# Softmax row sums of an attention layer: from products with ones on TensorE to a pass through DRAM, GpSimd additions and VectorE block transposes

## The chip, the cores and the metric

The kernel runs on one core of a Trainium2 chip. The time is the device time of one execution in microseconds (us). A core has five engines that run side by side, each taking its own instructions strictly in order: TensorE (PE, matmuls into PSUM), VectorE (DVE), ScalarE (ACT), GpSimd (POOL) and SyncE (SP), which here only issues transfers (DMA). PEld is PE's loading of weights.

## The reference

Two graph layers, each with a layer norm and a ReLU ahead and a residual around it, on 64 batches of 256 tokens with 512 features, in float32. The change concerns the second one, masked attention with 8 heads of 64:

```python
q = split_heads(h @ Wq.T + bq)
k = split_heads(h @ Wk.T + bk)
v = split_heads(h @ Wv.T + bv)
scores = jnp.einsum('bhqd,bhkd->bhqk', q, k) * scale
scores = jnp.where(mask, -jnp.inf, scores)
attn = jax.nn.softmax(scores, axis=-1)
out = jnp.einsum('bhqk,bhkd->bhqd', attn, v)
out = out.transpose(0, 2, 1, 3).reshape(b, n, D_MODEL)
return out @ Wo.T + bo
```

The first layer is a graph attention with one head: `e` is a sum of a column and a row term, goes through a leaky ReLU, the mask and a softmax, and weighs `h = X W`; its output is the weighted `h` beside `h` itself.

## The kernel before

The 64 batches are worked in 32 groups `g` of two batches `b`. All programs are unrolled Python loops. A software pipeline interleaves four things: the attention of batch (g,b), the output product of the batch before it, the q, k and v products of group g+1, and the first layer and norms of groups g+2 and g+3. One turn of this pipeline is called a stage (g,b) here.

The main loop (line 940 on) reads the order of each stage from a string. `S` issues the scores, `m` masks one pair of heads, `u` takes a piece of the projections of g+1 (`project`), `o` a piece of the output product (`outputs`), `s` a piece of the first layer (`first_layer`), `n` a piece of the first norm (`first_norm`). Each stage starts with `weigh`, which finishes the batch before, and then with `scores`.

PE's matmuls are held in exactly the order in which the program writes them (`in_order`, line 131). On the other engines a scheduler may move instructions, except that `not_sooner` (line 123) puts one behind the last one that was recorded on its engine. An engine then works in that fixed order: an instruction that waits holds up all behind it.

The steps around the change:

- `scores` (line 755): per head two matmuls per 128 keys into a PSUM bank, then ACT's exponential into `p` (128 keys by head, key half and 256 queries). The banks come from a ring of five (`mm`, line 109), which `ph`, `po`, `pr`, `total` and others share.
- `mask_pairs` (line 780): DVE multiplies a pair of heads by the mask; POOL then adds the second key half into the first, `p[:, :, 0, :] += p[:, :, 1, :]`, so that sums over keys need one half only.
- `value_differences` (line 750): POOL subtracts in `v` the first key half from the second, which makes up for that addition in the product with `v`.
- `weigh` (line 799): PE multiplies ones by `p` into `total`: for each query the sum over keys, 4 heads in the 4 blocks of 32 partitions, each block holding 32 equal rows. DVE takes the reciprocal `r`. PE multiplies `v` by `p` into `pr`, one bank for four heads, and DVE writes `oT = pr * r`. DVE then makes sums of the parts of `oT` for a seven-product (Strassen-like) form of the output product.
- `outputs` (line 836): seven products `py`, each added into `x` by DVE. Three use one bank held for them, the rest the ring.
- `project` (line 675): the same seven products for q, k and v; ACT keeps some results (`kept_q`, `kept_k`, `kept_v`) before PE adds to the same bank, DVE adds others.
- `first_layer` (line 552): `ph` matmuls, ACT's copy to `H`, POOL's addition into `x`; a row passed through DRAM (`rows`, `line`, `own`); `e` by ACT, DVE and ACT again; the mask; `po` matmuls, DVE's normalising, the statistics (`stats`: `st`, `mv`) and the norm of the second layer.
- `norm_T` (line 414): the factors of a norm (DVE, then POOL's power), ACT's `xn`, DVE's 32x32 block transposes `xt`, a transfer to DRAM (`passed`) and four back (`moved`), and ACT's copy to `hT`. It is a transposition by DVE's blocks and a trip through DRAM.
- `residual` (line 658): POOL adds the output bias into `x`.

All transfers of the loop are issued on SP. The tiles `p`, `r` and `e` lie in one pool; `p` and `r` have one buffer, `e` has two; `hT0` has one.

Of the kernel before, what the change touches and what calls it, by code (L numbers as in the profile page):

```python
# [57 lines left out]
def bounded(  # L58
# [350 lines left out]
            vector.bn_stats(st, src[t])  # L409
        vector.bn_aggr(mv[:, t, :], st)  # L410

    put_last, sums_last = [], []

    def norm_T(src, mv, name, by_pe):

        factor, xn, passed, turned = {}, {}, {}, {}
        J = P // S  # L420

        def factors(b):
            tiles = slice(b * NT, (b + 1) * NT)
            several = small.tile([P, 3, NT], F32, tag="factor", name=f"factor{name}_{b}")
            ve, less, rstd = (several[:, i, :] for i in range(3))
            vector.tensor_scalar(ve, mv[:, tiles, 1], EPS, None, op0=ALU.add)
            vector.tensor_scalar(less, mv[:, tiles, 0], -1.0, None, op0=ALU.mult)
            if name == "0_0":
                not_sooner(gpsimd, "tensor_tensor", rstd, ve, rexp, op=ALU.pow)
            else:  # L430
                gpsimd.tensor_tensor(rstd, ve, rexp, op=ALU.pow)
            gpsimd.tensor_tensor(less, less, rstd, op=ALU.mult)
            factor[b] = less, rstd

        def norm(b):
            less, rstd = factor[b]
            for t in range(NT):
                r = b * NT + t
                xn[r] = att.tile([P, D], F32, tag="xn", name=f"xn{name}_{r}", bufs=2)
                operands = dict(bias=less[:, t : t + 1], scale=rstd[:, t : t + 1])  # L440
                if scalar.last:
                    last = scalar.last
                    taken = scalar.activation(xn[r], src[r], AF.Relu, **operands)
                    for other in [last, *put_last] if name == "0_2" else [last]:
                        after(taken, other)
                else:
                    scalar.activation(xn[r], src[r], AF.Relu, **operands)

        def turn(b):
            tiles = range(b * NT, (b + 1) * NT)  # L450
            if by_pe:
                for t in tiles:
                    turned[t] = mm(f"pt{name}_{t}").rearrange("p (c n) -> p c n", c=HP)
                    for c in range(HP):
                        transpose(turned[t][:, c, :], xn[t][:, c * P : (c + 1) * P], ident)
                return

            xt = att.tile([P, J, HP, NT, S], F32, tag="xt", name=f"xt{name}_{b}", bufs=1)
            passed[b] = dram.tile([P, J, HP * NT * S], F32, tag="passed", name=f"passed{name}_{b}")
            for t in tiles:  # L460
                not_sooner(
                    vector, "transpose",
                    xt[:, :, :, t % NT, :], xn[t].rearrange("p (c j a) -> p j c a", j=J, a=S),
                )
            sync.dma_start(passed[b], xt.rearrange("p j c t n -> p j (c t n)"))

        def fetch(b):
            if by_pe:
                return
            moved = att.tile([P, J, HP, NT, S], F32, tag="moved", name=f"moved{name}_{b}")  # L470
            for j in range(J):
                nc.sync.dma_start(  # L472
                    moved[j * S : (j + 1) * S].rearrange("a i c t n -> a i (c t n)"),
                    passed[b].rearrange("(i a) j e -> j a i e", a=S)[j],
                )
            for t in range(NT):
                turned[b * NT + t] = moved[:, :, :, t, :].rearrange("p i c n -> p c i n")

        def put(b, dst):
            for t in range(NT):  # L480
                to = dst[:, :, t * P : (t + 1) * P]
                if not by_pe:
                    to = to.rearrange("p c (i n) -> p c i n", n=S)
                not_sooner(scalar, "copy", to, turned[b * NT + t])
            put_last[:] = [scalar.last]

        return factors, norm, turn, fetch, put
# [64 lines left out]
    def first_layer(g):  # L552

        xt = [xs[g, b][:, t, :] for b in range(GB) for t in range(NT)]
        for r in range(GT):
            b, t = divmod(r, NT)
            ph = mm(f"ph_{g}_{r}")[:, : F1 + 2]
            for c in range(HP):
                matmul(
                    ph, hT0[g, b][:, c, t * P : (t + 1) * P], w0_sb[:, c, :],  # L560
                    start=(c == 0), stop=(c == HP - 1),
                )
            scalar.copy(H[:, r, : F1 + 2], ph)
            gpsimd.tensor_add(xt[r][:, F1:], H[:, r, 2 : F1 + 2], xt[r][:, F1:])
            if r < GT - 1:
                yield

        pT = {}
        if g:

            rows = small.tile([P, GT, 8], F32, tag="rows", name=f"rows_{g}", bufs=2)
            not_sooner(vector, "transpose", rows.rearrange("p t c -> p (t c)"), H[:, :, 0:8])
            line = dram.tile([P // 8, S], F32, tag="line", name=f"line_{g}")
            nc.sync.dma_start(line, rows.rearrange("p t c -> p (t c)")[::8, :])
            own = att.tile([P, P // S, GT, S], F32, tag="r", name=f"own_{g}", bufs=1)
            nc.sync.dma_start(
                own.rearrange("p k t j -> p (k t j)"),
                line.rearrange("(o k) j -> o (k j)", o=1).to_broadcast([P, TOK]),
            )
            own = own.rearrange("p k t j -> p t k j")  # L580
            yield
        else:
            yield
            pn = mm(f"pn_{g}")
            for t in range(GT):
                transpose(pn[:, t * P : (t + 1) * P], H[:, t, 0:1].to_broadcast([P, P]), ident)
            own = pn.rearrange("p (t k j) -> p t k j", t=GT, j=S)
        for b in range(GB):
            e = pT[b] = att.tile([P, NT, N], F32, tag="e", name=f"e_{g}_{b}")
            for kb in range(NT):  # L590
                not_sooner(
                    scalar, "activation",
                    e[:, kb, :].rearrange("p (t k j) -> p t k j", t=NT, j=S),
                    own[:, b * NT : (b + 1) * NT], AF.Identity,
                    bias=H[:, b * NT + kb, 1:2], scale=1.0,
                )
# [158 lines left out]
    def scores(g, b):  # L755
# [6 lines left out]
        for i in range(HP):  # L762
# [9 lines left out]
            for j in range(2):  # L772
                last = scalar.last
                made = scalar.activation(pair[:, j], sc[j], AF.Exp, scale=scale)
                for other in [last, *put_last] if g == b == 0 and i > 1 else [last]:
                    after(made, other)
        places.extend((q_tag, k_tag))
        return p
# [1 line left out]
    def mask_pairs(p, last_group):  # L780


        for i in range(HP):
# [10 lines left out]
                after(made, other)  # L794
            yield

    oTs = {}

    def weigh(g, b, p):
# [1 line left out]

        v, v_tag = qkv["v", g, b]
        name = f"{g}_{b}"
        total = mm(f"total_{name}").rearrange("p (q n) -> p q n", q=NQ)
        r = att.tile([P, NQ, N], F32, tag="r", name=f"r_{name}", bufs=1)
        for quad in range(NQ):
            blocks = range(1 if g < NG - 1 else NT)
            for kb in blocks:
                for j in range(QH):
                    matmul(  # L810
                        total[j * S : (j + 1) * S, quad, :], ones, p[:, quad * QH + j, kb, :],
                        start=(kb == 0), stop=(kb == blocks[-1]),
                    )
        for quad in range(NQ):
            not_sooner(vector, "reciprocal", r[:, quad, :], total[:, quad, :])
        for quad in range(NQ):
            pr = mm(f"pr_{name}_{quad}").rearrange("p (h n) -> p h n", h=2)
            for half in range(2):
# [17 lines left out]
    def outputs(g, b):  # L836
# [41 lines left out]
        if g == NG - 1:  # L878
            nc.sync.dma_start(og[g, b][:, 0, D // 2 :], xt[:, 0, D // 2 :])
        else:  # L880
            nc.sync.dma_start(og[g, b], xt)
        yield


# [52 lines left out]
    run(verdict)  # L937


    steps = ("Smmnuuuumonmuossnuussounounonosuo", "Ssmmususuososmuomssusuonusonuouunous")  # L940
    waiting, late = None, iter(())
    for g in range(NG):
        products = project(g + 1) if g + 1 < NG else iter(())
        pieces = first_layer(g + 2) if g + 2 < NG else iter(())
        for b, parts in enumerate(steps):
            if g == b == 0:

                parts = "Smmnnuuuumnnmussnussuunununsu"
            elif g == 0 or g == 1 and b == 0:

                parts = "Ssmmususuososmuomssusuonusouuouous" if b else "Snn" + parts[1:]
            if waiting is not None:
                weigh(*waiting)
                late = outputs(*waiting[:2])
            for i, part in enumerate(parts):
                if part == "u":
                    next(products, None)
                elif part == "o":
# [4 lines left out]
                    next(norms, None)  # L963
                elif part == "m":
                    next(masks)
                else:
                    waiting = (g, b, scores(g, b))
                    masks = mask_pairs(waiting[2], g == NG - 1)
                if i == (len(parts) * 3 // 4, 6)[b] and g < NG - 1:
                    value_differences(g, b)  # L970
                if i == len(parts) // 2:
                    if g == b == 0:
                        weight_sums("o")
                    if g == max(NG - 2, 0) and b == 1:
# [380 lines left out]
```

## Time and profile before

| | |
|---|---|
| median of three runs | 2475.68 us (2475.18 to 2477.83) |
| span of the profiled execution | 2476.3 us |
| POOL's `p` additions | 248 of 1623 ns |
| DVE's mask products `p` | 256 of 1342 ns |
| DVE's reciprocals `r<-total` | 128 of 1727 ns |
| PE's `total<-p,ones` | 1056 records of 128x32 weights, 256 columns |
| granted TensorE clock | 0.999 |
| DMA | 213.58 MB, 26% of 16 engines' time |

The span is that of one profiled execution; the median comes from runs beside it. Busy time is the sum over an engine's instructions; PE's records overlap, since matmuls are pipelined, so that the mean of one is longer than the time it adds. Each float32 matmul leaves two records.

A line of the timeline gives start and duration in us, engine, line of the code (35 is the helper that records every instruction, 137 the matmul helper), operation, output and inputs, shapes and count; in brackets stands the idle time of the engine just before, and what ended it.

### The profile page before, as it was taken

The numbers are of one execution on the slowest core, as the hardware profiler recorded it, in microseconds if no ns is written. First come the engines' busy times: TensorE is split into PE (matmuls) and PEld (weight loads), VectorE is DVE, ScalarE is ACT, GpSimd is POOL, SyncE is SP. The second block draws the span as 40 slices with busy tenths as digits, with TensorE's granted clock in tenths as the row PEclk, the third lists the DMA queues.
The fourth block names the chain that finished last, engine by engine and source line by source line (L and its number), as shares of the span: only waits on it lengthen the run. The fifth ranks groups of instructions, "written<-read, shape, count | busy, mean of one in ns | idle before, by whom it ended". The sixth has DMA issues, their size and how long they took to land.

```text
span 2476.3 us, 41327 instructions
## 1 busy us (share of the span) xinstructions
PE 2453.9 (99%) x16044; PEld 2037.4 (82%) x16044; DVE 1690.3 (68%) x3006; ACT 1010.0 (41%) x2017; POOL 1000.8 (40%) x964
## 2 busy tenths in 40 slices
PE   8999999999999999999999999999999999999998
PEld 7788888888888888888888888888888888888886
DVE  6677666676766776666767667676677666676656
ACT  4544344443443444444434434444434344343431
POOL 2533444433444334444334453344443344433430
PEclk9999999999999999999999999999999999999999
DMA  6222223232232322232322323222222223232100
GB/s 191 77 86 79 84 81 99 86 103 78 72 99 81 103 79 84 82 99 86 99 77 73 103 81 103 79 84 82 94 90 93 78 73 107 80 105 80 52 32 36
DMA packets 135129, 213.58 MB, mean 86 GB/s; under 512 B 15504, under 2 KB 80272, under 8 KB 134928
## 3 DMA queue, kind: packets, MB, share of 16 engines
q1 hardware_dynamic: 134928, 210.89, 26.3%
q8 instruction: 128, 2.10, 0.4%
q14 instruction: 73, 0.60, 0.1%
HBM read 112.20 MB, written 98.63 MB: 85 GB/s over the span
## 4 chain that ended last, share of the span: by engine, by line
PE 97%; DMA 1%; DVE 1%; ACT 0%; issue 0%; SPq 0%; POOL 0%; DVEq 0%
PE pq L137 16%; PE pk L137 16%; PE py L137 15%; PE pv L137 15%; PE sc L137 10%; PE ph L137 9%; PE pr L137 9%; PE po L137 4%; PE total L137 3%; DMA w_sb<-in_L_gnn_W_dram 0%; DMA moved<-passed 0%; DMA passed<-xt 0%; DVE p L35 0%; SPq L472 0%; DVE r L35 0%
## 5 line engine op out<-in xcount | busy, mean ns | idle before, releaser
L35 POOL TENSOR_TENSOR p<-p 128x512 f32<-128x512 f32 x248 | 398.9, 1623 | 676.6 <-DVE p L35 675.3
L35 ACT ACTIVATE p<-sc 128x512 f32<-128x512 f32 x512 | 258.0, 624 | 236.5 <-PE sc L137 232.6
L35 DVE TENSOR_TENSOR p<-p,maskT 128x1024 f32<-128x1024 f32 x256 | 338.3, 1342 | 1.2 <-ACT p L35 1.2
L35 DVE TENSOR_TENSOR x<-py,x 128x256 f32<-128x256 f32 x448 | 186.4, 416 | 166.5 <-PE py L137 157.7
L35 ACT ACTIVATE xn<-x,factor 128x512 f32<-128x512 f32 x256 | 194.5, 808 | 211.4 <-POOL factor L35 211.3
L35 DVE RECIPROCAL r<-total 128x256 f32<-128x256 f32 x128 | 215.7, 1727 | 91.7 <-PE total L137 91.7
L137 PE MATMUL py<-wo_sb,oT 128*128 128x256 f32 x1024 | 262.5, 379 | 0.9 <-DVE oT L35 0.6
L137 PE MATMUL sc<-q,k 64*128 64x256 f32 x2048 | 252.2, 388 | 1.0 <-ACT p L35 1.0
L137 PEld LDWEIGHTS sc<-q,k 64*128 64x128 f32 x2048 | 211.2, 186 | 42.5 <-issue 26.3
L137 PE MATMUL pk<-hT,wk_sb 128*128 128x256 f32 x1024 | 244.8, 382 | 0.0
L137 PE MATMUL pq<-hT,wq_sb 128*128 128x256 f32 x1024 | 239.9, 382 | 0.0
L137 PE MATMUL ph<-w_sb,hT 128*128 128x258 f32 x1024 | 236.8, 384 | 1.5 <-DVE prod L35 1.2
L137 PE MATMUL pv<-wv_sb,hT 128*128 128x256 f32 x1024 | 237.0, 379 | 0.4 <-ACT kept_v L35 0.4
L35 POOL TENSOR_TENSOR factor<-factor,rexp 128x2 f32<-128x2 f32 x128 | 90.6, 708 | 353.9 <-DVE factor L35 353.9
L137 PE MATMUL pr<-p,v 128*32 128x256 f32 x4096 | 232.7, 379 | 0.0
L137 PEld LDWEIGHTS ph<-w_sb,hT 128*128 128x128 f32 x1024 | 195.2, 191 | 32.6 <-ACT hT L35 2.3
L137 PEld LDWEIGHTS pk<-hT,wk_sb 128*128 128x128 f32 x1024 | 192.3, 190 | 35.5 <-issue 10.4
L137 PEld LDWEIGHTS pq<-hT,wq_sb 128*128 128x128 f32 x1024 | 191.8, 190 | 35.3 <-issue 9.9
L137 PEld LDWEIGHTS py<-wo_sb,oT 128*128 128x128 f32 x1024 | 194.1, 190 | 28.9 <-DVE oT L35 1.1
L137 PEld LDWEIGHTS pv<-wv_sb,hT 128*128 128x128 f32 x1024 | 194.4, 190 | 27.2 <-ACT kept_v L35 0.8
L137 PEld LDWEIGHTS pr<-p,v 128*32 128x32 f32 x4096 | 133.1, 110 | 87.9
L137 PE MATMUL py<-wo_sb,o_sums 128*128 128x256 f32 x768 | 197.4, 379 | 0.9 <-DVE x L35 0.9
(125 smaller groups left out, 3637.0 us busy)
## 6 DMA issues: line engine op xcount, KB each, us to landing
passed<-xt SPq DMA_DIRECT2D x124, 512.0 KB, 2.7
moved<-passed SPq DMA_DIRECT2D x496, 128.0 KB, 3.1
x<-in_x_dram SPq DMA_DIRECT2D x64, 512.0 KB, 4.2
out_dram<-x SPq DMA_DIRECT2D x62, 512.0 KB, 3.1
own<-line SPq DMA_DIRECT2D x31, 256.0 KB, 3.1
wq_sb<-in_L_gnn_Wq_dram SPq DMA_DIRECT2D x2, 512.0 KB, 9.8
wk_sb<-in_L_gnn_Wk_dram SPq DMA_DIRECT2D x2, 512.0 KB, 11.0
wv_sb<-in_L_gnn_Wv_dram SPq DMA_DIRECT2D x2, 512.0 KB, 7.4
```

What stands on the lines that cost most here:

```text
L35: instruction = getattr(self.engine, operation)(*args, **kwargs)
L137: in_order(nc.tensor.matmul(*args, **kwargs))
```

## The change

The sums over keys no longer come from PE. For all groups but the last, a new generator `fold` does them in six pieces, called by a new letter `f` in the strings:

1. the first four heads of `p` (first key half, into which POOL has added the second) are written to DRAM (`put`), and read back so that each block of 32 partitions holds one head (`fetch`: four transfers; partition a of the block gets keys a, 32+a, 64+a, 96+a),
2. the second four heads are written to DRAM,
3. POOL adds the four keys of a partition in two additions,
4. DVE transposes the 32x32 blocks and sums each block's 32 keys (`sum_up`); the second four heads are read back,
5. POOL's additions for these,
6. DVE's transposes and sum for these, and a reciprocal of the 16 sums in each partition.

`weigh` then spreads the reciprocals back over partitions with one block transpose of a broadcast input. The read-back data `parts` borrows the buffer of `e` (for b = 0) or of `hT0` (for b = 1); the two `e` tiles of a group become one tile `both` of the same size. In the strings of b = 1 some `m` stand earlier. A few instructions are held behind others (`not_sooner`, `norm_last`) that were free before.

```diff
-    put_last, sums_last = [], []
+    put_last, norm_last, sums_last = [], [], []
...
                     scalar.activation(xn[r], src[r], AF.Relu, **operands)
+            norm_last[:] = [scalar.last]
...
-                nc.sync.dma_start(
+                sync.dma_start(
                     moved[j * S : (j + 1) * S].rearrange("a i c t n -> a i (c t n)"),
...
-            gpsimd.tensor_add(xt[r][:, F1:], H[:, r, 2 : F1 + 2], xt[r][:, F1:])
+            if g < 2:
+                gpsimd.tensor_add(xt[r][:, F1:], H[:, r, 2 : F1 + 2], xt[r][:, F1:])
+            else:
+                not_sooner(
+                    gpsimd, "tensor_add", xt[r][:, F1:], H[:, r, 2 : F1 + 2], xt[r][:, F1:]
+                )
...
+        both = att.tile([P, GB, NT, N], F32, tag="e", name=f"e_{g}", bufs=1)
         for b in range(GB):
-            e = pT[b] = att.tile([P, NT, N], F32, tag="e", name=f"e_{g}_{b}")
+            e = pT[b] = both[:, b]
...
-                for other in [last, *put_last] if g == b == 0 and i > 1 else [last]:
+                if g == b == 0:
+                    others = [last, *put_last] if i > 1 else [last]
+                else:
+                    others = [last, *put_last, *norm_last]
+                for other in others:
                     after(made, other)
...
+    row_sums = {}
+
+    def fold(g, b, p):
+        if g == NG - 1:
+            return
+        compact = small.tile([P, NQ, N // S], F32, tag="compact", name=f"compact_{g}_{b}", bufs=2)
+        row_sums[g, b] = compact
+        pool, tag = (att, "e") if b == 0 else (big, "hT0")
+        rows = []
+
+        def put(quad):
+            rows.append(dram.tile([P, QH, N], F32, tag="rows", name=f"rows_{g}_{b}_{quad}"))
+            heads = slice(quad * QH, (quad + 1) * QH)
+            not_sooner(sync, "dma_start", rows[quad], p[:, heads, 0, :])
+
+        def fetch(quad):
+            parts = pool.tile([P, P // S, N], F32, tag=tag, name=f"parts_{g}_{b}_{quad}", bufs=1)
+            for j in range(QH):
+                not_sooner(
+                    sync, "dma_start", parts[j * S : (j + 1) * S],
+                    rows[quad][:, j, :].rearrange("(i a) n -> a i n", a=S),
+                )
+            return parts
+
+        def add(parts):
+            not_sooner(gpsimd, "tensor_add", parts[:, :2], parts[:, :2], parts[:, 2:])
+            gpsimd.tensor_add(parts[:, 0], parts[:, 0], parts[:, 1])
+
+        def sum_up(quad, parts):
+            not_sooner(vector, "transpose", parts[:, 1], parts[:, 0])
+            vector.reduce_sum(
+                compact[:, quad], parts[:, 1].rearrange("p (k a) -> p k a", a=S), axis=AX.X
+            )
+
+        put(0)
+        parts = fetch(0)
+        yield
+        put(1)
+        yield
+        add(parts)
+        yield
+        sum_up(0, parts)
+        parts = fetch(1)
+        yield
+        add(parts)
+        yield
+        sum_up(1, parts)
+        vector.reciprocal(compact, compact)
+        yield
...
-        total = mm(f"total_{name}").rearrange("p (q n) -> p q n", q=NQ)
         r = att.tile([P, NQ, N], F32, tag="r", name=f"r_{name}", bufs=1)
-        for quad in range(NQ):
-            blocks = range(1 if g < NG - 1 else NT)
-            for kb in blocks:
-                for j in range(QH):
-                    matmul(
-                        total[j * S : (j + 1) * S, quad, :], ones, p[:, quad * QH + j, kb, :],
-                        start=(kb == 0), stop=(kb == blocks[-1]),
-                    )
-        for quad in range(NQ):
-            not_sooner(vector, "reciprocal", r[:, quad, :], total[:, quad, :])
+        if (g, b) in row_sums:
+            compact = row_sums.pop((g, b)).rearrange("p q k -> p (q k)")
+            not_sooner(
+                vector, "transpose", r.rearrange("p q (k a) -> p (q k) a", a=S),
+                compact[:, :, None].to_broadcast([P, NQ * N // S, S]),
+            )
+        else:
...
-            nc.sync.dma_start(og[g, b], xt)
+            not_sooner(sync, "dma_start", og[g, b], xt)
...
-    steps = ("Smmnuuuumonmuossnuussounounonosuo", "Ssmmususuososmuomssusuonusonuouunous")
+    steps = ("Smmfnuuuumonmfuofssfnuufssoufnounonosuo", "Ssmmfusmusmfuososfuosfsusuonufsonufouunous")
...
-                parts = "Smmnnuuuumnnmussnussuunununsu"
+                parts = "Smmfnnuuuumnnmfufssfnussfuununfunsu"
...
-                parts = "Ssmmususuososmuomssusuonusouuouous" if b else "Snn" + parts[1:]
+                parts = "Ssmmfusmusmfuososfuosfsusuonufsoufuouous" if b else "Snn" + parts[1:]
...
+                elif part == "f":
+                    next(folds, None)
+                    continue
                 else:
                     waiting = (g, b, scores(g, b))
                     masks = mask_pairs(waiting[2], g == NG - 1)
+                    folds = fold(*waiting)
```

The branch behind the last `else` of `weigh` is the code of before, for the last group. Positions in a string that start other work (the value differences, the residual, the loads) are counted without the `f`.

## The prediction

> **What bounds the kernel now.** I read the page's busy shares and its chain that ended last, then the chain in order of time for one group of two batches, then the timeline where TensorE (PE) meets the other engines.
>
> ```profile
> PE 2453.9 (99%) x16044; PEld 2037.4 (82%) x16044; DVE 1690.3 (68%) x3006; ACT 1010.0 (41%) x2017; POOL 1000.8 (40%) x964
> ...
> PE 97%; DMA 1%; DVE 1%; ACT 0%; issue 0%; SPq 0%; POOL 0%; DVEq 0%
> ```
>
> PE is never without work, so only PE's own work and new PE waits change the time. The chain in order of time at a stage's start:
>
> ```profile
> 1072.27 1.00 PE total L137 x16
> 1073.27 3.45 PE pr L137 x64
> 1076.72 3.85 PE sc L137 x32
> ```
>
> `total`, the products with ones, costs 1.00 us and follows without a gap. A stage (g,1) lasts 37.0 us (1035.26 to 1072.27), a stage (g,0) 38.8 (1072.20 to 1110.98 in the timeline). The timeline at the end of stage (g,0) shows how early the others are:
>
> ```profile
> 1102.80 0.69 DVE L35 BATCH_NORM_STATS2 st<-x 128x6 f32<-128x512 f32 x1
> ...
> 1104.78 0.71 POOL L35 TENSOR_TENSOR factor<-factor,rexp 128x2 f32<-128x2 f32 x1 [2.10 <-DVE factor L35]
> ...
> 1105.72 1.28 POOL L35 TENSOR_TENSOR v<-v 128x512 f32<-128x512 f32 x1
> ...
> 1106.84 0.69 DVE L35 TENSOR_TENSOR k<-pk,kept_k 128x512 f32<-128x512 f32 x1 [1.37 <-PE pk L137]
> ...
> 1109.50 1.27 DVE L35 SCALAR_TENSOR_TENSOR e<-e 128x512 f32<-128x512 f32 x2
> ...
> 1110.98 1.07 PE L137 MATMUL total<-p,ones 128*32 128x256 f32 x16
> ...
> 1111.87 3.64 PE L137 MATMUL pr<-p,v 128*32 128x256 f32 x64
> 1112.12 3.37 DVE L35 RECIPROCAL r<-total 128x256 f32<-128x256 f32 x2 [0.61 <-PE total L137]
> ...
> 1115.41 1.22 DVE L35 TENSOR_TENSOR oT<-pr,r 128x512 f32<-128x512 f32 x2
> ...
> 1116.60 4.03 ACT L35 ACTIVATE p<-sc 128x512 f32<-128x512 f32 x8 [4.50 <-PE sc L137]
> ```
>
> The statistics (`st`) start 8.2 us before PE's `total`; POOL's `v` difference, which `pr` reads, ends at 1107.0, 4 us early. In the middle of stage (g,1):
>
> ```profile
> 1055.85 0.24 DVE L35 TENSOR_SCALAR factor<-mv 128x2 f32<-128x2 f32 x2
> ...
> 1057.10 1.52 ACT L35 ACTIVATE xn<-x,factor 128x512 f32<-128x512 f32 x2 [0.36 <-POOL factor L35]
> 1057.21 1.18 DVE L35 TENSOR_TENSOR p<-p,maskT 128x1024 f32<-128x1024 f32 x1
> ...
> 1058.53 0.56 ACT L35 COPY kept_v<-pv 128x512 f32<-128x512 f32 x1
> ...
> 1060.88 1.89 PE L137 MATMUL pv<-wv_sb,sums 128*128 128x256 f32 x8
> ```
>
> Here ACT's `kept_v` must be done before PE's next `pv`, which adds to the same bank: it ends 1.6 us before that product's first weight load (1060.67). These two leads are what the change can use up. Last, the transfers that the new ones resemble (the DMA view; the last number is us to landing):
>
> ```profile
> passed<-xt SPq DMA_DIRECT2D x124, 512.0 KB, 2.7
> moved<-passed SPq DMA_DIRECT2D x496, 128.0 KB, 3.1
> ```
>
> [...] the first `o_sums` takes 0.42 us at 1040.87 with POOL idle, 1.51 at 1077.88 with POOL adding. [...] `xt<-xn`, 512 elements, takes 686 ns against 682 for `bn_stats` over 512, so a transpose costs what a plain pass does.
>
> **The change part by part.**
>
> Removed: 62 of the 64 `total` products (the last group keeps its own) and 124 reciprocals of 1727 ns. PE's 16 records are worth 16 x 3.45/64 = 0.86 us, at the pace of `pr`'s 64 in 3.45, of the 1.00; the other 0.14 is the switch to 32-column tiles (PEld waits 0.33 us on "issue" before `total`), which `pr` now pays. I take 0.86; the bound is 1.00. So 62 x 0.86 = 53.5 us (at most 62). At the program's end the chain also holds a `DVE r` of 1.82 us once; about 2 us go there.
>
> Added on DVE per batch: two transposes of 128x256 and two sums (0.42 us each, by the 128x256 additions; the trace has none of that shape), a reciprocal of 16 columns (0.18, by the 128x1 `ri` of 0.164), one broadcast transpose of 128x512 (0.69, by `xt`[...]). That is 2.6 us against 3.45 removed, so DVE does not become the bound. POOL: two additions of 128x512 (1.3 to 1.6) and two of 128x256 (0.7), 4.3 us a batch, 62 x 4.3 = 267: POOL goes to 51%. DMA: 2 MB a batch, 127 MB on 214: its share 26% to about 42%. SP issues 10 more transfers a batch; a fetch's four take 1.75 us to issue, as `moved` does.
>
> Does the round trip arrive? Stage (g,0), counted from its start: masked pair two is added by POOL at about 12; put lands 15.2; the fetch issues to 17.1 and lands 20 (3.1 from the last issue); POOL adds to 22.3; DVE sums to 23.3, in a hole that before is 4.8 us long (DVE `q` waits for PE). The second fetch waits for that sum (one `parts` buffer): issue 25.1, landing 28; POOL, which has four `x<-x,b_out` of 1.25 first, adds to 31.1; DVE sums from 32.3. The `moved` transfers queued on SP behind the first put and fetch land by 21, needed near 22. In (g,1) all is met with 2 us or more to spare. Transfers are hidden; their cost comes through engine order.
>
> *First wait, (g,0) to (g,1).* In the order in which the built program issues DVE's instructions, the next group's `st` no longer precede `k` (1102.80, before 1106.84): they stand behind the second sum, `k` and the reciprocal. Nothing hides that, since `k` waits for PE's `pk`, 4.14 us before stage end. From stage end: `k` ends -3.45, reciprocal -3.25, two `st`, two `mv` and two `x` additions (0.69, 0.18, 0.42 each) to -0.6, `factor` to -0.3; POOL's power and product (0.71 + 0.20 and gaps) to +0.67, and behind them on POOL, in order, the `v` difference of 1.27, to +1.95. PE's `pr` reads the changed `v` at +0.57 (switch 0.14, then four products of the unchanged half, eight records, 0.43). PE waits 1.4. The same lateness runs on by ACT (`xn` +2.2, `e` +3.95) and DVE (`e` +4.7, new `r` +5.4, first `oT` +6.1), where the fourth score bank, which takes over `pr`'s first bank, is due at 4.8: also 1.4, in parallel, not in addition. I take 1.45 (0.8 to 2.2).
>
> *Second wait, in (g,1).* PE is now 1.45 - 0.86 = 0.6 us later than before relative to the stage's start. DVE leaves `oT` at 6.75 instead of 5.57. Two mask products of 1.2 are moved ahead of the statistics: the second `factor` ends at 20.83 + 1.2 + 2.4, less 0.9 of waiting (0.49 and 0.45 before `ri`) that vanishes, plus 0.4[...]: 23.9. POOL 0.9, ACT `xn` 1.52, and in ACT's order behind it `kept_v` 0.56: 27.0. PE wants it at 1060.67 - 1035.19 + 0.6 = 26.1. Wait 1.0 (0 to 2). The first `sum_up`, held by POOL's addition behind that `factor`, and `x` for `py` come about 0.4 late, covered by this wait.
>
> Each wait recurs where statistics of a following group exist, about 29 of 31 groups. Sum: 2476.3 - 53.5 - 2 + 29 x 2.45 = 2491.8. The median lies 0.6 below the profiled span: 2491.
>
> **The rivals.**
> A, PE stays dense: 2476 - 53.5 to - 62, that is 2414 to 2423. For it: DVE loses 0.85 us a batch. Against: the order above gives away an 8.2 us lead.
> B, ending faster: the first wait stands, but ACT's `kept_v` comes in time, since the shift of DVE in (g,1) is partly hidden (its waits for PE are longer than I read). Then 2476 - 55.5 + 29 x 1.45 = 2463. It decides from the point where `kept_v` ends below 26.1; break-even is 55.5/29 = 1.9 us of waits a group.
> C, the round trip is slower than unloaded transfers suggest, with 42% DMA and two 512 KB moves at once: (g,0)'s second sum has about 1 us of spare time; 1.5 us lost per group on top gives 2491 + 45 = 2535.
> D, waits and saving cancel: 2471 to 2481.
>
> **How the numbers follow.** Forecast 50% (2481 to 2520); C 20%; D 8%; B 12%; A 10%. Bounds: saving 53.5 to 62, waits 0.8 to 4.2 a group, so 2438 to 2545 at the extremes; I take 2448 to 2545, which leaves A and a part of C out; the forecast's own is 2481 to 2520. With 0.2% (5 us) as the least that can be told from no change: faster 0.22, same 0.08, slower 0.70.
>
> **What would show it.** Right: PE idle before `pr` waiting on POOL `v` (or before `sc` on DVE `oT`), about 1.4 us each second stage; PE idle before `pv` on ACT `kept_v`; stages (g,0) near 37.9 us (38.8 - 0.86) and (g,1) near 38.6 (37.0 - 0.86 + 2.45); `r` transposes at 0.7 us. Wrong: PE at 99% without waits (A); PE or ACT waiting on DMA `parts` or `moved` (C); `st` still early.

## The result and the profile after

| | before | after |
|---|---|---|
| median, us | 2475.62 (2475.18 to 2477.83, 4 runs) | 2496.82 (2495.93 to 2497.92, 4 runs) |
| ratio | | 1.0084, 95% interval 1.007 to 1.0099 |
| span of the profiled execution, us | 2476.3 | 2495.1 |

The changed kernel is 0.8% slower; the forecast was 2491, in a range of 2448 to 2545. First the page of the kernel after: the lines of busy time and of the chain that ended last.

```profile
PE 2414.9 (97%) x15052; PEld 2003.1 (80%) x15052; DVE 1671.8 (67%) x3254; ACT 1011.9 (41%) x2017; POOL 1293.4 (52%) x1212
...
PE 60%; POOL 12%; DVE 11%; DMA 10%; issue 4%; SPq 3%; ACT 0%; POOLq 0%; DVEq 0%; ACTq 0%
```

PE is busy 39.0 us less and still ends 19 us later. Its share of the chain fell from 97% to 60%: the end of the program is now set by a path that leaves PE and returns to it in each group. What PE waits for is in the view of waits (PE's own; us in total, times, longest):

```profile
PE ph L137 <- ACT hT L35: 34.6, 29, 10.2
PE pr L137 <- POOL v L35: 22.5, 28, 1.3
```

The second row is the wait before `pr` that was forecast. The first was not: PE waits for the first layer's input. The weight loads, which run ahead, show the same `pr` wait as 36.0 us in 28 times, 1.29 each. The chain in order of time, from the read-back of one (g,0) to `pr`, joins the two engines and the transfers:

```profile
1105.90 3.17 DMA parts<-rows
...
1109.19 1.27 POOL parts L35
...
1111.25 5.60 POOL x L35 x6
...
1117.40 1.28 POOL parts L35
...
1119.50 0.46 DVE parts L35
...
1120.32 0.68 DVE k L35
1121.00 0.16 DVE compact L35
1121.16 0.55 DVE st L35
...
1123.14 0.25 DVE factor L35 x2
...
1124.37 1.24 POOL v L35
...
1125.66 0.40 PE pr L137
```

The statistics `st`, which belong to the group after next and have nothing to do with these sums, stand in DVE's fixed order behind the second sum, `k` and the compact reciprocal; POOL's `v` difference stands behind the `factor` that they make. The transfers take about as long as forecast (from issue to landing 3.5 us for the put and 3.0 for one of the fetch, in the median), but they start 4 us later, for a reason that comes below: the fetch lands at 1109.1, POOL is busy from there to the second sum, and everything behind it is late. The unexpected wait is seen on SP's queue (timeline of the same stage, 0.43 us for each transfer issued) beside ACT's copy and PE's matmuls:

```profile
1101.01 0.53 SPq L35 DMA_DIRECT2D rows<-p  x1
1101.63 1.56 SPq L35 DMA_DIRECT2D moved<-passed  x2
1104.60 1.73 SPq L35 DMA_DIRECT2D parts<-rows  x4
1106.37 0.91 SPq L35 DMA_DIRECT2D moved<-passed  x2
...
1110.46 1.14 ACT L35 COPY hT<-moved 128x512 f32<-128x512 f32 x2 [3.43 <-DMA moved<-passed]
...
1111.13 3.75 PE L137 MATMUL ph<-w_sb,hT 128*128 128x258 f32 x16 [1.06 <-ACT hT L35]
```

The data of `moved` were in DRAM from about 1098 (`passed` was issued at 1095.42). All four transfers stood behind the put, which waits for POOL's addition in `p`, and two of them behind the whole fetch, which waits for the put to land. In the very first stage the same order costs more, since `moved` of two batches stands behind the put: ACT's `hT` comes at 114.97 and PE waits 10.23 us.

Counted from a stage's first `sc` to the next stage's (us; (g,0) and (g,1) are means over 29 groups):

| kernel | first stage | (g,0) | (g,1) |
|---|---|---|---|
| before | 36.66 | 38.83 | 37.01 |
| after | 48.59 | 40.06 | 36.14 |
| e6, without the sums | 35.79 | 37.93 | 36.15 |
| e9, reordered | 36.65 | 37.95 | 36.34 |

So the changed kernel gains 0.87 us in (g,1), the whole of what was to be gained there, and loses 1.23 in (g,0) and 11.9 in the first stage. 29 x (1.23 - 0.87) + 11.9, less 0.86 in the second stage, is 21.5. The first `sc` starts 3.5 us sooner in the profile of after (90.5 and 94.0 us), which leaves 18.0 of the 18.8 by which the spans differ.

### The profile page after: what moved, and what is told of

It reads as the page before. It is cut to its first block, busy times and chain, and to the rows that moved or that the text cites. A ratio compares the mean times of both kernels' runs of the same rounds, so it can differ in the third digit from the quotient of the medians.

```text
span 2495.1 us, 41066 instructions
## 1 busy us (share of the span) xinstructions
PE 2414.9 (97%) x15052; PEld 2003.1 (80%) x15052; DVE 1671.8 (67%) x3254; ACT 1011.9 (41%) x2017; POOL 1293.4 (52%) x1212
## 3 DMA queue, kind: packets, MB, share of 16 engines
q8 instruction: 120, 1.97, 0.3%
## 4 chain that ended last, share of the span: by engine, by line
PE 60%; POOL 12%; DVE 11%; DMA 10%; issue 4%; SPq 3%; ACT 0%; POOLq 0%; DVEq 0%; ACTq 0%
PE pv L137 15%; PE pk L137 10%; PE py L137 9%; PE pr L137 9%; PE sc L137 6%; DMA parts<-rows 5%; PE po L137 4%; POOL parts L35 4%; PE pq L137 4%; POOL p L35 4%; DMA rows<-p 3%; SPq L35 3%; DVE o_sums L35 2%; PE ph L137 2%; POOL x L35 2%
## 5 line engine op out<-in xcount | busy, mean ns | idle before, releaser
L35 POOL TENSOR_TENSOR p<-p 128x512 f32<-128x512 f32 x248 | 409.9, 1670 | 418.9 <-DVE p L35 417.7
L35 POOL TENSOR_TENSOR parts<-parts 128x512 f32<-128x512 f32 x248 | 247.8, 999 | 231.4 <-DMA parts<-rows 220.9
L35 DVE TENSOR_TENSOR p<-p,maskT 128x1024 f32<-128x1024 f32 x256 | 345.4, 1370 | 1.2 <-ACT p L35 1.2
L35 POOL TENSOR_TENSOR factor<-factor,rexp 128x2 f32<-128x2 f32 x128 | 120.2, 939 | 317.7 <-DVE factor L35 317.6
L137 PE MATMUL ph<-w_sb,hT 128*128 128x258 f32 x1024 | 243.1, 391 | 34.7 <-ACT hT L35 34.6
L137 PE MATMUL pr<-p,v 128*32 128x256 f32 x4096 | 240.0, 381 | 22.5 <-POOL v L35 22.5
L35 DVE STREAM_TRANSPOSE parts<-parts 128x256 f32<-128x256 f32 x124 | 54.9, 443 | 295.8 <-POOL parts L35 295.7
L137 PEld LDWEIGHTS pr<-p,v 128*32 128x32 f32 x4096 | 123.9, 110 | 129.0 <-POOL v L35 36.0
```

The costliest lines, as they stand in the source:

```text
L35: instruction = getattr(self.engine, operation)(*args, **kwargs)
L137: in_order(nc.tensor.matmul(*args, **kwargs))
```

## The experiments

Each begins from the kernel after, if nothing else is said. Ratios are to the kernel before on the same chip.

**e1: the `v` difference earlier.**

```diff
-                if i == (count * 3 // 4, 6)[b] and g < NG - 1:
+                if i == (count * 2 // 3, 6)[b] and g < NG - 1:
```

> POOL's v difference of batch 0 is issued two steps earlier, ahead of the norm factors instead of behind them; nothing else moves on POOL. Theory (two waits with one root, the late statistics, stand in parallel): pr no longer waits for POOL, but the first oT still ends about 0.9 us after the fourth score bank is due, so that PE waits there instead; gain 28 x 0.35 = 10 us, 2487. Rival (the v difference alone is the wait): all of 28 x 1.25 us goes, 2462.

Measured 2493.82, ratio 1.0066 (1.0052 to 1.008). The `pr` wait is gone, and only 3 us are gained for 28 waits (the intervals of the two ratios overlap). In its place PE waits for DVE's first `oT` within `sc` (23 times, 8.1 us in all), (g,1) takes 36.92 instead of 36.14, and the `ph` wait grows from 34.6 to 40.1 us. The wait behind it ran in parallel, as the prediction's first step said.

**e2: `moved` ahead of the first put.**

```diff
-    steps = ("Smmfnuuuumonmfuofssfnuufssoufnounonosuo", "Ssmmfusmusmfuososfuosfsusuonufsonufouunous")
+    steps = ("Smmnfuuuumonmfuofssfnuufssoufnounonosuo", "Ssmmfusmusmfuososfuosfsusuonufsonufouunous")
...
-                parts = "Smmfnnuuuumnnmfufssfnussfuununfunsu"
+                parts = "Smmnnuuuumnnfmfufssfnussfuununfunsu"
```

> In stage (g,0) the piece that fetches moved is written ahead of the first put and fetch, so on SP's queue all moved transfers stand in front of them; in stage (0,0) the first f comes after both such pieces. Theory (order on SP): the waits of ph for ACT's hT go, 10 to 12 us once at the start and about 27 x 0.85 = 23 us later: 2462. Rival (the transfers are late because 45% DMA load stretches them all): ph waits as before, 2492 to 2502. Second rival (put and fetch are now later and the sums miss their slot): slower than 2497.

Measured 2535.33, ratio 1.0234 (1.022 to 1.0248). No `ph` wait is left, so the cause was SP's order. But PE now arrives sooner at the end of (g,0) while the second sum does not, and the scheduler moved that sum behind `k` on DVE: the `pr` wait is 2.02 us nearly every time. And it costs more than it lasts. The timeline and the windows (columns: the window and its length, then the busy time of PE, PEld, DVE, ACT and POOL, the granted clock, DMA share, GB/s) after one such wait:

```profile
1144.21 4.92 PE L137 MATMUL pr<-p,v 128*32 128x256 f32 x56 [2.02 <-POOL v L35]
```
```profile
1144.00:1145.00 1.00, 0.79 (x16) 0.53 (x20) 1.00 (x2) 1.00 (x3) 0.16 (x1) 1.00 0.00 0
1145.00:1146.00 1.00, 1.00 (x24) 0.53 (x18) 0.91 (x2) 1.00 (x3) 0.00 (x0) 0.77 0.00 0
1146.00:1147.00 1.00, 1.00 (x16) 0.58 (x12) 0.89 (x3) 0.83 (x3) 0.00 (x0) 0.50 0.91 356
1147.00:1148.00 1.00, 1.00 (x16) 0.45 (x9) 0.90 (x2) 0.48 (x1) 0.00 (x0) 0.50 0.95 379
1148.00:1149.00 1.00, 1.00 (x12) 0.22 (x4) 0.23 (x1) 0.00 (x0) 0.00 (x0) 0.53 0.84 313
1149.00:1150.00 1.00, 1.00 (x12) 0.88 (x10) 0.77 (x2) 0.00 (x0) 0.00 (x0) 1.00 0.00 0
```

These 56 records take 4.92 us; after a wait that leaves the clock alone (e11, below) they take 3.23. From within 1145 to within 1148 the granted clock is 0.50, for 3.40 us by the shares of these four windows (0.46 + 1 + 1 + 0.94), and the records take 1.69 us more, on top of the wait.

**e3: the statistics ahead of the second sum.**

```diff
-    steps = ("Smmfnuuuumonmfuofssfnuufssoufnounonosuo", "Ssmmfusmusmfuososfuosfsusuonufsonufouunous")
+    steps = ("Smmfnuuuumonmfuofssfnuufssounfounonosuo", "Ssmmfusmusmfuososfuosfsusuonufsonufouunous")
```

> The last f of stage (g,0) (second sum_up and reciprocal) is written behind the piece with the statistics, so DVE makes the statistics in its idle time ahead of the second sum. Theory: factor, v difference, xn, e and oT are all in time again, the pr wait goes and none takes its place: 2497 - 28 x 1.25 = 2462, with the ph waits unchanged. Rival (the second sum, now later, makes r and oT late): sc waits for DVE oT about 1 us each, 2490 or more.

Measured 2492.51, ratio 1.007 (1.0057 to 1.0084). The `pr` wait is gone, which shows that the place of `st` made it. A new one stands before `py`, 28 times 0.85 us (the timelines of PE, DVE and POOL):

```profile
1121.70 1.13 PE L137 MATMUL py<-wo_sb,o_sums 128*128 128x256 f32 x4 [0.85 <-DVE x L35]
```
```profile
1119.71 0.45 DVE L35 STREAM_TRANSPOSE parts<-parts 128x256 f32<-128x256 f32 x1 [3.58 <-POOL parts L35]
```
```profile
1115.43 0.71 POOL L35 TENSOR_TENSOR factor<-factor,rexp 128x2 f32<-128x2 f32 x1 [0.66 <-DVE factor L35]
1116.22 0.19 POOL L35 TENSOR_TENSOR factor<-factor 128x2 f32<-128x2 f32 x1
1116.37 1.27 POOL L35 TENSOR_TENSOR v<-v 128x512 f32<-128x512 f32 x1
1117.60 2.07 POOL L35 TENSOR_TENSOR parts<-parts 128x512 f32<-128x512 f32 x2
```

POOL now makes `factor` and `v` first, its additions for the sum start 2.8 us later, counted from `pr` (35.15 and 32.34), and DVE's sum, waiting for them, holds up an addition into `x` that PE needs. The rival was right on the time: one of three coupled places was mended.

**e4: no sums at all, and e6: the same in the order of the kernel after.** Both begin from the kernel before; `total`, the reciprocals and the transfers are left out for all groups but the last, and `oT` is `pr` times one. e6 adds to e4 the change's constraint on ACT:

```diff
+            norm_last[:] = [scalar.last]
...
-                for other in [last, *put_last] if g == b == 0 and i > 1 else [last]:
+                if g == b == 0:
+                    others = [last, *put_last] if i > 1 else [last]
+                else:
+                    others = [last, *put_last, *norm_last]
+                for other in others:
```

> The kernel of before without any row sums in all groups but the last: no total products, no reciprocals, no division (oT is pr times a one). It is the time of PE alone, if nothing takes the removed products' place. Theory: 62 x 0.86 and about 2 us at the end go: 2420. If the switch of tile width went with total: 62 x 1.00, 2412. If more than 2430, other waits stand behind total.

> As e4_no_sums (no row sums and no reciprocals for all groups but the last; the division of the softmax is left out), with the one constraint of the kernel after kept: ScalarE's exponentials of p do not go ahead of the xn and hT activations before them. Theory: e4's wait before sc came from ScalarE's order alone; with it gone TensorE is dense and the time is the floor that the change could reach, 2476 - 62 x 0.87 = about 2422 (2413 to 2428), with no wait of TensorE over 0.5 us that recurs. Rival: leaving the sums out uncovers another wait whatever the order, then 2450 or more, and rows of waits on ACT or DVE in every group.

e4: 2530.22, ratio 1.0218 (1.0204 to 1.0232), slower with less work. e6: 2420.55, ratio 0.9773 (0.976 to 0.9787). In e4 ACT's order (its timeline) put `hT` and `xn` between the first exponential and the others, and PE's fourth score bank waited, in 23 of 28 groups with the halved clock behind it (16 records of `pq` in 5.41 us instead of 3.72):

```profile
1093.17 0.60 ACT L35 ACTIVATE p<-sc 128x512 f32<-128x512 f32 x1 [4.12 <-PE sc L137]
...
1094.69 1.52 ACT L35 ACTIVATE xn<-x,factor 128x512 f32<-128x512 f32 x2
1096.12 3.50 ACT L35 ACTIVATE p<-sc 128x512 f32<-128x512 f32 x7
```
```profile
1096.75 1.61 PE L137 MATMUL sc<-q,k 64*128 64x256 f32 x8 [1.80 <-ACT p L35]
1098.29 5.41 PE L137 MATMUL pq<-hT,wq_sb 128*128 128x256 f32 x16
```

With the constraint no wait recurs. e6 is what the change could give if nothing else came late: 2477.19 - 2420.55 = 56.6 us.

**e5: the first batch by ones.**

```diff
-        if g == NG - 1:
+        if g == NG - 1 or g == b == 0:
             return
```

with `total` over one key half for that batch, as before.

> The kernel after, but for the first batch (0,0) alone the row sums are taken by products with ones as before, without the pass through DRAM. Theory: in the first stage the transfers moved_2_0 and moved_2_1 stand on SP's queue behind the first put, which waits for GpSimd, and this alone makes the PE wait of 10.23 us before ph at 115.6 us; it goes, the first stage falls from 48.6 us to about 37.5, and 0.86 us of products and nothing else is added: 2497 - 11 + 1 = about 2486. Every later stage stays as in the kernel after. Rival: the wait at the start has another cause (GpSimd's or ScalarE's order), then the first stage stays over 46 us and the time at 2495 to 2498.

Measured 2488.56, ratio 1.0048 (1.0034 to 1.0062). The first stage falls from 48.59 to 36.65 and the PE wait of 10.23 is gone; later stages are as in the kernel after (40.12 and 36.14). The stall at the start is the put's place on SP's queue. The difference of the medians to the kernel before falls from 21.2 to 11.4 us, by 9.8 of the 11 expected.

**e8: without the way through DRAM.** POOL adds straight from `p`, so that sums of other elements than the row's come out, and an addition of 1 stands for the reciprocal.

```diff
-            not_sooner(sync, "dma_start", rows[quad], p[:, heads, 0, :])
+            rows[quad] = p[:, heads, 0, :]
...
-            not_sooner(gpsimd, "tensor_add", parts[:, :2], parts[:, :2], parts[:, 2:])
+            not_sooner(gpsimd, "tensor_add", parts[:, :2], own[:, :2], own[:, 2:])
...
-        vector.reciprocal(compact, compact)
+        vector.tensor_scalar(compact, compact, 1.0, None, op0=ALU.add)
```

> The kernel after without the pass through DRAM: GpSimd adds straight from p, so the sums are of the wrong elements, and an addition of 1 stands for the compact reciprocal; every engine instruction keeps its size and count, and 18 transfers a group (20 MB over SP in all per 10 groups) are left out. Theory: the engines' own added work costs nothing, the price is the time of the round trip (about 6.5 us each way of put and fetch) and its place on SP: ph waits and the start's stall go, and most of the pr wait, 2425 to 2445. Rival: GpSimd's and VectorE's added instructions are themselves what is late, then 2465 or more with the pr wait still there.

(The text on record miscounts: 20 transfers and 4 MB a group are left out.) Measured 2427.34, ratio 0.9803 (0.979 to 0.9817), 7 us over e6. All of DVE's and POOL's added instructions are there and no PE wait recurs after the first group. This kernel also has another order: with the sums early, the scheduler puts `st` ahead of `k`. So it shows that the added engine work fits, not that transfers alone are the price.

**e7 and e9: all places at once.**

```diff
-            if name == "0_0":
+            if name[0] == "0":
                 not_sooner(gpsimd, "tensor_tensor", rstd, ve, rexp, op=ALU.pow)
...
-            nc.sync.dma_start(line, rows.rearrange("p t c -> p (t c)")[::8, :])
+            not_sooner(sync, "dma_start", line, rows.rearrange("p t c -> p (t c)")[::8, :])
...
         put(0)
+        yield
         parts = fetch(0)
...
-    steps = ("Smmfnuuuumonmfuofssfnuufssoufnounonosuo", "Ssmmfusmusmfuososfuosfsusuonufsonufouunous")
+    steps = ("Smmfnfuuuumonmfuofssfnuufssounfounonosuo", "Ssmmffusmusmfuososfuosfsusuonufsonufouunous")
...
-                if i == (count * 3 // 4, 6)[b] and g < NG - 1:
+                if i == (count // 3, 6)[b] and g < NG - 1:
```

with e5's edit, and the same extra `f` in the strings of the first stages.

> The kernel after with four changes of order and no change of work: the four fetch transfers issued after the moved transfers that already wait (put and fetch are two pieces), the next group's statistics ahead of the second sum, GpSimd's second parts addition ahead of the factor and the v difference at a third of the stage, line behind the second fetch; and (0,0) by ones as in e5. Theory: the pr wait (about 1.25 us a group), the ph wait (0.85) and the start's stall (10) are all order and nothing of them is the price of the pass itself: 2497 - 29 x 2.1 - 10 = 2426 (2420 to 2445). Rival: the waits run in parallel with others behind them, as e1 to e3 each showed, and TensorE waits for oT before sc, for x before py or for the sums: 2460 to 2500.

Measured 2442.41, ratio 0.9864 (0.9849 to 0.9879): the `pr` and `ph` waits are gone and none of their size took their place in later groups (what is left shows in (g,1), which takes 36.43 us in the mean, 0.29 more than in the kernel after). One new wait of 5.35 us stood in the first stage, where `factor` in program order came behind four additions of POOL. e9 keeps `factor` in order from group 3 on only:

```diff
-            if name[0] == "0":
+            if name == "0_0" or name[0] == "0" and int(name[2:]) > 2:
```

> e7_all_ordered, but GpSimd's factor is kept in program order only for the statistics of group 3 and later; for groups 1 and 2 it may go ahead of the four hT additions again. Theory: in e7 ScalarE's xn waited 4.33 us for that factor (100.67 us, behind four GpSimd additions of 1.3) and kept_q behind it, which made the PE wait of 5.35 us at 104 us; it goes, the first stage falls from 44.1 us to about 36.7, and 2442 becomes about 2435. Rival: another wait takes its place in the first stage (ScalarE's hT from moved), then the time stays over 2439.

Measured 2431.74, ratio 0.9815 (0.9802 to 0.9829), faster than both kernels: 45 us under before, 11 over e6. Its page, and SP, DVE and POOL in one (g,0) (timeline; `pr` of the stage before starts at 1054.86):

```profile
PE 2407.2 (99%) x15068; PEld 2008.5 (83%) x15068; DVE 1711.2 (70%) x3250; ACT 1008.9 (41%) x2017; POOL 1285.5 (53%) x1208
...
PE 93%; DVE 2%; DMA 2%; POOL 1%; issue 1%; ACT 1%; SPq 0%; POOLq 0%; ACTq 0%; DVEq 0%
```
```profile
1070.26 0.52 SPq L35 DMA_DIRECT2D rows<-p  x1
1070.88 2.56 SPq L35 DMA_DIRECT2D moved<-passed  x4
1073.85 1.73 SPq L35 DMA_DIRECT2D parts<-rows  x4
```
```profile
1084.60 0.68 DVE L35 BATCH_NORM_STATS2 st<-x 128x6 f32<-128x512 f32 x1
```
```profile
1073.93 1.26 POOL L35 TENSOR_TENSOR v<-v 128x512 f32<-128x512 f32 x1
...
1087.02 2.07 POOL L35 TENSOR_TENSOR parts<-parts 128x512 f32<-128x512 f32 x2
```

`moved` goes out in the 3.1 us in which SP would only wait for the put to land, at no cost to the fetch; `v` is done 17.6 us before the next `pr` (1092.78); `st` starts 8.2 us before it, where in the kernel after it starts 3.2 before (1121.08 and 1124.31). POOL and DVE are about as busy as in the kernel after (1285.5 and 1711.2 us, there 1293.4 and 1671.8).

**e10: only the small edits.** Every batch by ones, the rest of the change kept.

```diff
-        if g == NG - 1:
+        if True:
             return
```

> The kernel after with the row sums of every batch by products with ones as before; what is left of the change is its smaller edits (one e tile for both batches, the x additions on GpSimd in program order, the exponentials behind xn, the moved transfers on record). Theory: these cost and bring nothing in themselves, 2474 to 2479. Rival: they cost part of what the kernel after lost, 2482 or more.

Measured 2477.39, ratio 1.0001 (0.9992 to 1.0009). The constraints and the shared `e` tile neither cost nor bring anything while the sums stay on PE.

**e11: put and fetch in two pieces, nothing else.**

```diff
         put(0)
+        yield
         parts = fetch(0)
...
-    steps = ("Smmfnuuuumonmfuofssfnuufssoufnounonosuo", "Ssmmfusmusmfuososfuosfsusuonufsonufouunous")
+    steps = ("Smmfnfuuuumonmfuofssfnuufssoufnounonosuo", "Ssmmffusmusmfuososfuosfsusuonufsonufouunous")
```

> The kernel after with only put and fetch as two pieces, so that moved transfers that already wait are issued between them (for later groups; the start stays as it is). Theory: the ph wait (0.85 us a group) goes, but TensorE then reaches the stage's end that much sooner while the second sum comes no sooner, and in VectorE's order the statistics stand behind three additions to x as well: the pr wait grows to about 2 us and the time does not fall, 2490 to 2540 (over 2510 if the waits reach 1.8 us, from where e2 and e4 showed the granted clock fall to half). Rival: the two waits are independent and the ph wait is simply saved: 2497 - 25 = 2472.

Measured 2530.5, ratio 1.0211 (1.0197 to 1.0225). In the waits of PE:

```profile
PE pr L137 <- POOL v L35: 60.4, 28, 5.1
PE ph L137 <- ACT hT L35: 10.6, 2, 10.1
```
```profile
1144.02 3.23 PE L137 MATMUL pr<-p,v 128*32 128x256 f32 x56 [2.69 <-POOL v L35]
```

The `ph` wait went but for the start, and the `pr` wait took its 24 us and more. The same edit is part of e9. What it brings depends on whether the path behind it has been shortened too.

## Why the prediction came out as it did

- **The saving** was right: 0.86 us a product, measured 0.87 in (g,1), 37.01 to 36.14, and 0.86 in (g,0) of e6, 38.78 to 37.92 in most stages. With the 2 us at the end, 55.5 was the sum; e6 gave 56.6.
- **The prices of the engines** hold where they were worked out: block transposes of 128x256 443 ns and sums 420 (0.42 forecast), the broadcast transpose 708 (690), POOL's additions 1270 and 729; the reciprocal of 16 columns 248 (180). DVE did not become the bound; POOL stands at 52% (51%), DMA at 45% (42%).
- **The first wait** was right in place, mechanism and nearly in size: 1.45 forecast, 1.29 on the weight loads, 28 times. That the `oT` wait runs beside it and not after it, e1 showed. That the place of `st` makes it, e3 showed.
- **The second wait**, ACT's `kept_v` before `pv` in (g,1), 1.0 us, did not come: (g,1) is 36.14 in the kernel after and 36.15 in e6. Counted from the stage's start, the forecast had `kept_v` done at 27.0 and needed at 26.1; in the medians of 28 groups it is done at 24.8 and needed at 25.6. The term that failed is DVE's second `factor`: it was to end at 23.9, which is 3.1 later than before, and ends at 21.8, which is 0.9 later. This step was wrong by its whole amount, 29 us.
- **"Transfers are hidden"** is the step that failed, in the sentence that the `moved` transfers behind the first put and fetch "land by 21, needed near 22". Counted from `pr` (1085.06), the put was issued at 15.95, not near 12, and ACT had `moved` at 25.4, where PE was ready at 25.0 (1111.13 - 1.06). The queue itself was in the forecast: `moved` stood behind the put and the fetch there too, and from the put to the landing it had 9 us, against 9.4 measured. What was mis-sized is the first term, that POOL has added the second masked pair "at about 12", for which no working was given. In the kernel before this addition ends at 15.1 from the stage's start (1072.20), which is 14.2 from `pr` (1073.09), and in the kernel after at 15.9 from `pr`; even in e6, which has no sums, it ends at 14.8 in the median. The lines of POOL, before and after:

```profile
1082.92 4.40 POOL L35 TENSOR_TENSOR p<-p 128x512 f32<-128x512 f32 x2 [3.81 <-DVE p L35]
```
```profile
1096.58 4.41 POOL L35 TENSOR_TENSOR p<-p 128x512 f32<-128x512 f32 x2 [2.68 <-DVE p L35]
```

  So some 2 to 3 us of the 4 are the forecast's figure, and 1.7 here (1.2 in the median) are new. The need was set too early as well, but by less: ACT would have had to start near 24.3, which is 25.0 less the 0.67 us from the start of its copy to `ph`. Part of the new delay is that POOL's four additions for `sums` now meet three instructions of DVE on `o_sums` and `oT` instead of one (timelines of DVE and POOL):

```profile
1089.98 1.38 DVE L35 TENSOR_TENSOR o_sums<-o_sums,oT 128x256 f32<-128x256 f32 x1
1091.28 1.49 DVE L35 TENSOR_TENSOR oT<-oT 128x256 f32<-128x256 f32 x1
1092.69 1.49 DVE L35 TENSOR_TENSOR o_sums<-oT,o_sums 128x256 f32<-128x256 f32 x1
```
```profile
1089.62 1.45 POOL L35 TENSOR_TENSOR sums<-sums,hT 128x512 f32<-128x512 f32 x1
1091.03 1.45 POOL L35 TENSOR_TENSOR hT<-hT 128x512 f32<-128x512 f32 x1
1092.44 1.46 POOL L35 TENSOR_TENSOR sums<-hT,sums 128x512 f32<-128x512 f32 x1
```

  These three took 0.42 us each in the kernel before, where only the first `o_sums` met POOL and took 1.51; here that one takes 0.42 and these take 1.38 to 1.49, one beside each instruction of POOL. POOL's three take 1.45 to 1.46 beside them, against 1.27 to 1.28 in the kernel before. What makes them longer beside each other, the traces do not show. Behind the late put the whole queue of SP is late: put and fetch wait at its head, and what is behind them waits with them. In e2 and e9, where `moved` does not stand behind the fetch, no such wait recurs. It cost about 24 us of `ph` waits (34.6 less 10.2) and 10.2 at the start, where the prediction had not looked at all; e5 took the latter away.
- **The time** came out near by luck, because two errors cancelled: 29 us of a wait that did not come against 24 and about 12 of one that was not foreseen. The forecast waits of 29 x 2.45 = 71 us stand against 29 x 2.13 (40.06 less 37.93) + 12.8 (48.59 less 35.79) = 75, both counted from e6.
- **The rivals:** A (2414 to 2423) did not come, for the reason that stood against it, the lead that the order gave away; e6 reaches it, and e9 comes within 9 us of it, in another order. B was right that `kept_v` comes in time, but not on the time. C's sign was right and its reason half so: not slow transfers (512 KB land in 3.5 us, 128 KB in 3.0) but their late start and their place in a queue. D (2471 to 2481) would have needed waits no larger than the saving; they were 75 against 56.6.

What stays open: the second sum's place in e7 and e9 was changed together with `factor` and `v`; which of them is enough with e11's edit was not tried, so it is not shown that every edit of e9 is needed. Nor were the put and fetch tried on another queue than SP's.

## What to carry to other kernels

When work leaves a bound engine for a path through several others, price the place of each new instruction in its queue, not only its duration, and take the time at which its input exists from the trace of the kernel before: the whole path here began 4 us later than was put down for it. e8 and e9 show that all of the added work fits; the change lost by order. Mending one place alone moved the wait to the next (e1, e3), made it worse (e2, e11) or took away one part (e5), and none of these came below the kernel before; several together did (e7, e9). A transfer that waited for data held up ready ones behind it (`moved`, in DRAM from about 1098, was issued at 1101.63 and 1106.37), so look at which ready transfers could be issued between a put and the fetch that needs it.

## What was not expected of the hardware

Waits of PE near 2 us cost nearly twice their length, 3.9 us, where the granted clock fell to 0.50 behind them (for 3.40 us in the windows shown with e2), and 2.2 us where it held. In e2 a stage (g,0) takes 40.15 us where the clock held after a wait of 2.02 and 41.83 where it fell, against 37.92 in most stages of e6. In e4 it takes 40.41 and 42.05 to 42.10. So e4's 28 waits cost 2.49 us each (the matmul records show 1.80, the weight loads 2.39), and the clock another 1.67 in 23 of them: 70 and 38 us, together 108 of the 110 by which e4 ends above e6.

Equal waits had unequal results: the clock fell after 23 of the 28 waits of 1.79 and 1.80 us in e4, and after 15 of the 22 of 2.01 to 2.03 in e2. The traces show what tells the two apart. All falls of one execution begin on one grid with a step of 3413.3 ns (25 falls in e2, 24 in e4, 20 in e11, each within 5 ns). The records of the clock show the same step in the two kernels compared: in the kernel before one stretch at 0.50 lasts 3413 ns (from 72.24 to 75.65 us), and in the kernel after the falls at 110.10 and 1646.10 us lie 1535997 ns apart, 450 steps. If the waits over 1 us in groups 1 to 29 are cut by this grid, the longest part within one step separates the two without an exception in these three runs:

| run, place of the wait | clock held | clock fell |
|---|---|---|
| e2, before `pr` | 7 waits, up to 1.98 us in one step | 21, from 2.01 up |
| e11, before `pr` | 12, up to 1.84 | 16, from 1.97 up |
| e4, within `sc` | 5, up to 1.27 | 23, from 1.28 up |

Two waits of 2.69 and 2.70 us in e11 were among those after which the clock held: a border of the grid lay within each. So in these runs it was the idle time within one step, and not the length of the whole wait, that went with a fall. Why 1.28 us within `sc` were enough, where before `pr` 1.98 were not, stays open.
